# Layer 3's attention in a four-layer kernel: keys before queries, transposes spread between the scores, values two heads behind

## The chip, the cores and the metric

The kernel runs on one NeuronCore of one Trainium2 chip. A NeuronCore has five engines that work side by side and wait for each other by semaphores: TensorE (PE) multiplies matrices and transposes, VectorE (DVE) and ScalarE (ACT) work element by element, GpSimd (POOL) takes odd jobs, and SyncE (SP) issues transfers. PE's products go to PSUM, a small memory of its own, from which DVE and ACT read them. Each engine has a queue of its own, with its instructions in the order in which they were built.

The metric is device time in microseconds (us) for one execution of the whole program. A profiled execution gives the records from which the profile and the trace are made.

## The reference

The reference is four transformer-like layers over 4 sequences of 512 tokens with 256 channels, all in 32-bit floating point. Each layer normalizes its input and adds an attention-like part and a feed-forward part to it. Layer 0 has a state-space mixer and a gated feed-forward, layer 1 a latent attention and a product-key lookup with a gated feed-forward, layer 2 a cheap head-mixing attention and eight small experts, and layer 3 the two parts that this document is about:

```
q = einsum('bpd,hde->bphe', x, W_Q) + b_Q       # 16 heads of 128
k = einsum('bpd,hde->bphe', x, W_K) + b_K
v = einsum('bpd,hde->bphe', x, W_V) + b_V
scores = where(causal, einsum('bqhe,bkhe->bhqk', q, k) / sqrt(128), -1e5)
attn = softmax(scores, axis=-1)
z = einsum('bkhe,bhqk->bqhe', v, attn)
out = einsum('bqhe,hed->bqd', z, W_O) + b_O
```

and a feed-forward of eight experts with 512 hidden units each, in which a router's softmax chooses, per token, the experts whose probabilities add up to 0.9. Here x is the normalized input of the layer.

## The kernel before, in words

The program is written in a tile language: the text allocates named tiles from pools and issues operations to engines, and a scheduler derives the semaphores, may move independent instructions of an engine against each other a little, and gives out the buffers. A pool tag with `bufs=2` has two buffers; a third tile of that tag has to wait until the first has been read for the last time. The PSUM banks are shared by three tags: "mm" with four buffers, "tr" (transposes) with two and "acc" (sums of products) with two.

What is computed concurrently is laid out by `weave`. Every stage is a Python generator that issues some instructions and then yields a number, its estimate of their cost. `weave` always continues the stream that has got the least far in its own total. In `layer3` the attention starts at 0 of its total of 765, and the experts (`top_p_experts`) start at 0.95: so the attention runs nearly alone, its last heads are woven with the experts' routers and first products, and the experts then run alone to the end.

`full_attention` (line numbers are those of the profile) goes through four groups `g` of four heads, and in each through the four sequences `b`. For one `g` and `b`:

- V for four heads is projected in four token tiles (L133, 128x512 each) and copied to SBUF by ACT (L1045).
- For each head, `project_heads` projects the queries and then the keys, each with two products of 512 columns (L125). DVE adds the bias to the queries and scales them (L1002), ACT adds the bias to the keys (L1005).
- `probabilities` is called for four blocks of 128 query tokens. Block i needs the first i+1 blocks of keys, so the score product (L577, in `exp_scores`) is 128, 256, 384 or 512 columns wide. DVE masks and takes each row's minimum in one pass (L580; the queries carry a negative scale, so the minimum is the maximum), ACT takes the exponential and its sum (L584), DVE takes the reciprocal of the sum (L1011) and scales the block (L1012). The tiles are called `pr0` to `pr3`.
- `values` belongs to the head before (the closure `behind`): its probabilities are transposed block by block on PE (L1023: 1, 2, 3 and 4 transposes of 128x128 into one "tr" buffer each), DVE copies each group to the tile PT (L1024), and four products of PT with V (L1027) add up z in an "acc" buffer, which ACT copies to `zT` with a bias (L1031).
- After the fourth head's values, `heads_out` multiplies `zT` by the output weights `wo` in four token tiles of four products each (L593), and DVE adds each to `x` (L142).

In a 32-bit product PE's records come in pairs, with a weight load (PEld) each; a transpose is one record. In the order in which the program before was built, PE does per head: the queries, the first of the keys' two products, the products with V of `values` (for the head two back by now), the second product of the keys, five of the ten transposes of the head before, the four scores, and the other five transposes; the scheduler has moved the pieces of `values` across the projections and the scores.

Of the kernel before, what the change touches and what calls it, by code (L numbers as in the profile page):

```python
# [14 lines left out]
P = 128  # L15
NB, SEQ, DM = 4, 512, 256
NT = NB * SEQ
NTILE = NT // P
TPB = SEQ // P
# [55 lines left out]
def v3(ap, b):  # L75
    return ap.rearrange("p (a b) -> p a b", b=b)
# [45 lines left out]
def project(c, out, w, cols, tokens):  # L122

    for d in range(2):
        c.nc.tensor.matmul(  # L125
            out, lhsT=w[:, d, cols], rhs=c.xnT[:, d, tokens], start=(d == 0), stop=(d == 1)
        )


def project_tokens(c, out, w, cols, tokens):  # L130

    for d in range(2):
        c.nc.tensor.matmul(  # L133
            out, lhsT=c.xnT[:, d, tokens], rhs=w[:, d, cols], start=(d == 0), stop=(d == 1)
        )


def add_scaled(c, t, part, w=None):

    x = c.x[:, t, :]  # L140
    if w is None:
        c.nc.vector.tensor_add(x, part, x)  # L142
    else:
        c.nc.vector.scalar_tensor_tensor(x, part, w, x, ALU.mult, ALU.add)  # L144
# [417 lines left out]
def late_mask(c, pool):  # L562

    late = c.tile(pool, [P, SEQ], "late")
    c.nc.vector.memset(late[:, : SEQ - P], 0.0)
    c.nc.vector.tensor_scalar_mul(late[:, SEQ - P :], c.neg, -1.0)
    return late


def exp_scores(c, pool, late, q, k, i, total, **kw):  # L570

    nc = c.nc
    n = (i + 1) * P
    sc = c.ps()[:, :n]
    nc.tensor.matmul(sc, lhsT=q[:, i * P : n], rhs=k[:, :n], start=True, stop=True)  # L577
    pr = c.tile(pool, [P, n], f"pr{i}", **kw)
    nm = c.tile(pool, [P, 1], "nm", bufs=4)
    nc.vector.tensor_tensor_reduce(  # L580
        out=pr, in0=sc, in1=late[:, SEQ - n :], scale=1.0, scalar=-NEG,
        op0=ALU.add, op1=ALU.min, accum_out=nm,
    )
    nc.scalar.activation(pr, pr, AF.Exp, bias=nm, scale=-1.0, accum_out=total)  # L584
    return pr


def heads_out(c, zT, wo, b):

    for t in range(TPB):  # L590
        po = c.ps("acc")[:, :DM]
        for h in range(4):
            c.nc.tensor.matmul(  # L593
                po, lhsT=zT[:, h, t * P : (t + 1) * P], rhs=wo[:, h, :],
                start=(h == 0), stop=(h == 3),
            )
        add_scaled(c, b * TPB + t, po)
# [5 lines left out]
def latent_pieces(c, a, keep, prep, open_pool):  # L603
# [147 lines left out]
    def turned(s, j):  # L751

        pt = c.ps("tr")
        n = SEQ - j * P
        for i in range(j, TPB):
            nc.tensor.transpose(  # L756
                pt[:, (i - j) * P : (i - j + 1) * P], prs[s][i][:, j * P : (j + 1) * P], c.ident
            )
        copy = nc.scalar.copy if j % 2 else nc.vector.tensor_copy
        return lambda: copy(PTs[s][:, START[j] : START[j] + n], pt[:, :n])  # L760
# [6 lines left out]
    for s in range(65):  # L767
        if s < 64:
            prs[s] = []
        for i in range(TPB):  # L770
            if s < 64:
                probabilities(s, i)
            if s > 0:
                if i == 0:
                    PTs[s - 1] = c.tile(pool, [P, 1280], "PT")
                ready, copy = copy, turned(s - 1, i)
# [200 lines left out]
def full_attention(c, a):  # L977

    nc, tc = c.nc, c.tc
    scale = 128.0 ** -0.5
    with ExitStack() as stack:
        keep, pool = (
            stack.enter_context(tc.tile_pool(name=name, bufs=bufs, side="right"))
            for name, bufs in (("f_keep", 1), ("f_h", 2))
        )
        bias = c.tile(keep, [P, 48 + DM], "bias")
        nc.sync.dma_start(bias, a["f_small"])
        late = late_mask(c, keep)  # L990
        for t in range(NTILE):
            nc.gpsimd.tensor_add(c.x[:, t, :], c.x[:, t, :], bias[:, 48:])

        def project_heads(w3, hh, b):

            wq, wk = w3[:2]
            tokens = slice(b * SEQ, (b + 1) * SEQ)
            cols = slice(hh % 4 * P, (hh % 4 + 1) * P)
            pq, pk = c.ps(), c.ps()
            project(c, pq, wq, cols, tokens)  # L1000
            q = c.tile(pool, [P, SEQ], "q")
            nc.vector.tensor_scalar(q, pq, bias[:, hh : hh + 1], -scale, ALU.add, ALU.mult)  # L1002
            project(c, pk, wk, cols, tokens)
            k = c.tile(pool, [P, SEQ], "k")
            nc.scalar.activation(k, pk, AF.Identity, bias=bias[:, 16 + hh : 17 + hh])  # L1005
            return q, k

        def probabilities(q, k, i):
            rinv = c.tile(pool, [P, 1], "rinv", bufs=4)
            pr = exp_scores(c, pool, late, q, k, i, rinv)  # L1010
            nc.vector.reciprocal(rinv, rinv)  # L1011
            nc.vector.tensor_scalar_mul(pr, pr, rinv)  # L1012
            return pr

        def values(prs, V, h, zT, hh):

            PT = c.tile(pool, [P, TPB, SEQ], "PT")
            for i, pr in enumerate(prs):
                n = (i + 1) * P
                pt = c.ps("tr")  # L1020
                for j in range(i + 1):
                    cols = slice(j * P, (j + 1) * P)
                    nc.tensor.transpose(pt[:, cols], pr[:, cols], c.ident)  # L1023
                nc.vector.tensor_copy(PT[:, : i + 1, i * P : n], v3(pt[:, :n], P))  # L1024
            z = c.ps("acc")
            for j in range(TPB):
                nc.tensor.matmul(  # L1027
                    z[:, j * P :], lhsT=V[:, j, h, :], rhs=PT[:, j, j * P :],
                    start=(j == 0), stop=(j == TPB - 1),
                )  # L1030
            nc.scalar.activation(zT[:, h, :], z, AF.Identity, bias=bias[:, 32 + hh : 33 + hh])  # L1031

        behind = None
        for g in range(4):
            w = c.unit(a["f_units"][g])
            w3 = [v3(w[:, i * 1024 : (i + 1) * 1024], 512) for i in range(3)]
            wo = c.tile(pool, [P, 4, DM], "wo")
            nc.sync.dma_start(wo, v3(a["f_out"][g], DM))
            for b in range(NB):
                V = c.tile(pool, [P, TPB, 4, P], "V")  # L1040
                for t in range(TPB):
                    tt = b * TPB + t
                    pv = c.ps()
                    project_tokens(c, pv, w3[2], slice(0, 512), slice(tt * P, (tt + 1) * P))
                    nc.scalar.copy(V[:, t, :, :], v3(pv, P))  # L1045
                    yield 1.7
                zT = c.tile(pool, [P, 4, SEQ], "zT")
                for h in range(4):
                    hh = 4 * g + h
                    q, k = project_heads(w3, hh, b)  # L1050
                    yield 3.4
                    prs = [probabilities(q, k, i) for i in range(TPB)]
                    yield 2.1
                    if behind:
                        yield behind()

                    def behind(prs=prs, V=V, h=h, zT=zT, hh=hh, wo=wo, b=b, g=g):
                        values(prs, V, h, zT, hh)
                        if h < 3:
                            return 3.2  # L1060
                        heads_out(c, zT, wo, b)
                        if g == 3:
                            c.part_done(b)
                        return 10.0
        behind()

# [147 lines left out]
def layer3(c, a):  # L1216
    weave(c, (full_attention(c, a), 765.0, 0.0), (top_p_experts(c, a), 765.0, 0.95))
# [200 lines left out]
```

## Time and profile before

| what | value |
|---|---|
| time, median of 3 runs (lowest, highest) | 3323.99 us (3313.49, 3325.25) |
| profiled execution: its own time | 3325.63 us |
| profiled execution: its span in the trace | 3323.9 us |
| PE, busy in the span | 3209.1 us (97%), 12524 records |
| DVE, busy in the span | 1894.4 us (57%) |
| ACT, busy in the span | 1255.3 us (38%) |
| layer 3's attention, first to last score (L577) in the trace | 1835.8 to 2676.2 us |
| mean granted TensorE clock | 0.99 |

The span is the time from the first to the last instruction of the profiled execution. A line of the profile's groups names the source line, the engine, the operation, the tiles written and read, the shapes and the number of records. In a timeline each line gives the start, the duration and the records merged into it, and in brackets how long the engine had been idle before and what released it. A table of windows gives the busy time of each engine in each stretch, then the granted clock of TensorE (1.00 is full speed), the share of the DMA engines and GB/s. Matmuls are pipelined, so that a record's end lies over the start of the next one, and the ends are modelled.

### The profile page before, as it was taken

The page shows a single profiled execution, that of the slowest core. Times are in us where ns is not written, and L with a number is a line of the kernel's source. Part 1 is how long each engine was busy: PE and PEld are TensorE (multiplying, and loading weights), DVE is VectorE, ACT ScalarE, POOL GpSimd, SP SyncE. Part 2 cuts the span into 40 slices and gives each one's busy share as a digit, 9 for nine tenths or more (in the row PEclk, how much of TensorE's full clock was granted, in tenths as well). Part 3 has the DMA queues.
Part 4 walks back from the last instruction along what each step waited for, and adds up shares of the span by engine and source line. Part 5 has one row for each costly group of instructions (what it writes and reads, how often), then busy time and mean ns, then how long its engine had stood idle before and what let it go on. Part 6 is the DMA issues. An engine that isn't in the chain of part 4 may idle for free.

```text
span 3323.9 us, 35406 instructions
## 1 busy us (share of the span) xinstructions
PE 3209.1 (97%) x12524; PEld 1921.4 (58%) x12524; DVE 1894.4 (57%) x4720; ACT 1255.3 (38%) x2870; POOL 579.8 (17%) x445
## 2 busy tenths in 40 slices
PE   8999999998899999999999999999999999999999
PEld 4556555655555555455655555556556665555555
DVE  4777778877788678656655545455455532222222
ACT  4444454443565645568322333333333311111111
POOL 0465556655212133100000000000000000000000
PEclk9999999998999999999999999999999999999999
DMA  3233323323213254301001000000000000000000
GB/s 124 77 105 96 125 85 105 102 96 115 59 43 98 50 146 127 90 14 42 15 1 53 5 1 26 0 20 7 0 20 1 1 19 19 20 21 20 17 0 26
DMA packets 75650, 165.14 MB, mean 50 GB/s; under 512 B 12368, under 2 KB 46288, under 8 KB 70608
## 3 DMA queue, kind: packets, MB, share of 16 engines
q1 hardware_dynamic: 64368, 127.20, 11.9%
q0 software_dynamic: 10240, 33.56, 4.1%
q8 instruction: 98, 1.61, 0.2%
q10 hardware_dynamic: 864, 2.12, 0.2%
q14 instruction: 80, 0.66, 0.1%
HBM read 149.08 MB, written 4.85 MB: 46 GB/s over the span
## 4 chain that ended last, share of the span: by engine, by line
PE 72%; DVE 12%; DMA 6%; issue 4%; POOL 4%; ACT 2%; SPq 0%; DVEq 0%; another core or an unknown queue 0%; POOLq 0%; ACTq 0%
PE mm L125 30%; PE acc L194 10%; PE mm L577 7%; PE mm L133 4%; PE acc L1027 4%; PE acc L593 3%; DMA G<-own 3%; DVE cy L259 2%; PE tr L1023 2%; DVE G L400 2%; DMA e<-in_p_experts,ids 2%; PE tr L756 1%; PE acc L813 1%; PE tr L486 1%; PE acc L800 1%
## 5 line engine op out<-in xcount | busy, mean ns | idle before, releaser
L125 PE MATMUL mm<-xnT,wu 128*128 128x512 f32 x2384 | 1083.4, 597 | 9.2 <-DVE cy L259 4.7
L125 PEld LDWEIGHTS mm<-xnT,wu 128*128 128x128 f32 x2384 | 444.8, 191 | 462.9 <-issue 426.4
L584 ACT ACTIVATE pr<-pr,nm 128x128 f32<-128x128 f32 (+3 forms) x512 | 286.6, 560 | 257.9 <-DVE nm L580 234.0
L186 ACT ACTIVATE sg<-mm 128x512 f32<-128x512 f32 x200 | 119.0, 595 | 697.7 <-PE mm L125 697.5
L187 DVE TENSOR_TENSOR hT<-sg,mm 128x512 f32<-128x512 f32 x200 | 136.9, 684 | 424.3 <-PE mm L125 415.3
L194 PE MATMUL acc<-wu,hT 128*128 128x256 f32 x1600 | 374.1, 382 | 0.0
L194 PEld LDWEIGHTS acc<-wu,hT 128*128 128x128 f32 x1600 | 300.7, 191 | 89.4 <-issue 34.8
L580 DVE CUSTOM_DVE_ANT_0 pr<-mm,late 128x128 f32<-128x128 f32 (+3 forms) x512 | 245.5, 486 | 70.4 <-PE mm L577 55.3
L125 PE MATMUL mm<-xnT,w_in 128*128 128x512 f32 x512 | 231.5, 596 | 6.6 <-DVE cy L259 5.1
L144 DVE SCALAR_TENSOR_TENSOR x<-acc,cw,x 128x256 f32<-128x256 f32 x256 | 123.3, 483 | 182.0 <-PE acc L194 177.1
L917 POOL DMA_INDIRECT e<-in_p_experts,ids x128 | 129.8, 1014 | 359.4 <-DVE x L144 315.1
L400 DVE TENSOR_TENSOR_SCAN G<-G,eye 128x1024 f32<-128x1024 f32 x64 | 155.6, 2431 | 56.4 <-DMA G<-own 56.3
L577 PE MATMUL mm<-kf,qf 128*128 128x128 f32 (+3 forms) x512 | 177.7, 448 | 7.8 <-DVE qf L735 4.4
L1024 DVE COPY PT<-tr 128x128 f32<-128x128 f32 (+3 forms) x256 | 118.7, 481 | 107.1 <-PE tr L1023 107.0
L426 POOL TENSOR_TENSOR G<-G,CB 128x1024 f32<-128x1024 f32 x64 | 151.1, 2361 | 142.2 <-ACT CB L352 81.3
L259 DVE SCALAR_TENSOR_TENSOR cy<-mm,ws,cy 128x509 f32<-128x509 f32 (+2 forms) x216 | 158.4, 741 | 28.9 <-ACT cy L255 25.6
L125 PEld LDWEIGHTS mm<-xnT,w_in 128*128 128x128 f32 x512 | 96.6, 191 | 111.0 <-issue 96.9
L412 ACT ACTIVATE xD<-xc,ws 128x128 f32<-128x128 f32 x256 | 84.3, 391 | 197.7 <-POOL y L449 191.7
L142 DVE TENSOR_TENSOR x<-acc,x 128x256 f32<-128x256 f32 x176 | 73.9, 421 | 148.1 <-PE acc L593 121.1
L577 PE MATMUL mm<-k,q 128*128 128x128 f32 (+3 forms) x512 | 154.9, 446 | 0.8 <-ACT k L1005 0.8
L1027 PE MATMUL acc<-PT,V 128*128 128x512 f32 (+3 forms) x512 | 148.8, 434 | 0.0
L1027 PEld LDWEIGHTS acc<-PT,V 128*128 128x128 f32 x512 | 97.4, 190 | 82.6 <-issue 32.7
(247 smaller groups left out, 4601.3 us busy)
## 6 DMA issues: line engine op xcount, KB each, us to landing
G<-own SPq DMA_DIRECT2D x64, 512.0 KB
w_in<-in_m_units SPq DMA_DIRECT2D x16, 1024.0 KB
eb<-since SPq DMA_DIRECT2D x96, 128.0 KB
wu<-in_o_units SPq DMA_DIRECT2D x8, 1536.0 KB
wo<-in_m_units SPq DMA_DIRECT2D x16, 512.0 KB
psw<-pes SPq DMA_DIRECT2D x128, 64.0 KB
wu<-in_g_units SPq DMA_DIRECT2D x4, 1536.0 KB
wu<-in_f_units SPq DMA_DIRECT2D x4, 1536.0 KB
```

The lines of the kernel that those rows point to most:

```text
L125: c.nc.tensor.matmul(out, lhsT=w[:, d, cols], rhs=c.xnT[:, d, tokens], start=(d == 0), stop=(d == 1))
L133: c.nc.tensor.matmul(out, lhsT=c.xnT[:, d, tokens], rhs=w[:, d, cols], start=(d == 0), stop=(d == 1))
L187: nc.vector.tensor_mul(h, sg, pu)
L194: nc.tensor.matmul(po, lhsT=hT[k][:, t * P : (t + 1) * P], rhs=wd[:, k, :], start=(i == 0), stop=(i == per - 1),)
L259: nc.vector.scalar_tensor_tensor(y[:, j:], src[:, : SEQ - j], conv[:, k, 3 - j : 4 - j], y[:, j:], ALU.mult, ALU.add,)
L400: nc.vector.tensor_tensor_scan(flat, flat, eye.rearrange("p h t -> p (h t)"), 0.0, ALU.mult, ALU.add)
L426: nc.gpsimd.tensor_mul(G, G, seqs[b][2][:, t, :][:, None, :].to_broadcast([P, HG, P]))
L577: nc.tensor.matmul(sc, lhsT=q[:, i * P : n], rhs=k[:, :n], start=True, stop=True)
L580: nc.vector.tensor_tensor_reduce(out=pr, in0=sc, in1=late[:, SEQ - n :], scale=1.0, scalar=-NEG, op0=ALU.add, op1=ALU.min, accum_out=nm,)
L584: nc.scalar.activation(pr, pr, AF.Exp, bias=nm, scale=-1.0, accum_out=total)
L917: nc.gpsimd.indirect_dma_start(out=e, out_offset=None, in_=a["p_experts"], in_offset=bass.IndirectOffsetOnAxis(ap=ids[:, t, k : k + 1], ax ...
L1027: nc.tensor.matmul(z[:, j * P :], lhsT=V[:, j, h, :], rhs=PT[:, j, j * P :], start=(j == 0), stop=(j == TPB - 1),)
```

## The change

`project_heads` is split into `keys` and `queries`, which are called in this order. `values` is split too: `turned` transposes one block of one head and has DVE copy it to PT, and what stays in `values` is the four products with V, ACT's copy to `zT` and, after the fourth head, `heads_out`.

Each head's round then runs so: the keys; the queries; the transposes of the last (512 wide) block of the head before; the products with V of the head two back; and then the four blocks' scores, with the transposes of blocks 2, 1 and 0 of the head before after the first, second and third score. The four blocks are no longer issued as one piece: after each the generator yields 0.7, where it yielded 2.1 after all four. The sum of the yields of four heads, with their V and `heads_out`, is 48.4 as before. After the last head what is left of the last two heads is done at the end.

```diff
@@ -991,19 +991,20 @@
         for t in range(NTILE):
             nc.gpsimd.tensor_add(c.x[:, t, :], c.x[:, t, :], bias[:, 48:])
 
-        def project_heads(w3, hh, b):
-
-            wq, wk = w3[:2]
-            tokens = slice(b * SEQ, (b + 1) * SEQ)
-            cols = slice(hh % 4 * P, (hh % 4 + 1) * P)
-            pq, pk = c.ps(), c.ps()
-            project(c, pq, wq, cols, tokens)
+        def queries(w3, hh, b):
+
+            pq = c.ps()
+            project(c, pq, w3[0], slice(hh % 4 * P, (hh % 4 + 1) * P), slice(b * SEQ, (b + 1) * SEQ))
             q = c.tile(pool, [P, SEQ], "q")
             nc.vector.tensor_scalar(q, pq, bias[:, hh : hh + 1], -scale, ALU.add, ALU.mult)
-            project(c, pk, wk, cols, tokens)
+            return q
+
+        def keys(w3, hh, b):
+            pk = c.ps()
+            project(c, pk, w3[1], slice(hh % 4 * P, (hh % 4 + 1) * P), slice(b * SEQ, (b + 1) * SEQ))
             k = c.tile(pool, [P, SEQ], "k")
             nc.scalar.activation(k, pk, AF.Identity, bias=bias[:, 16 + hh : 17 + hh])
-            return q, k
+            return k
 
         def probabilities(q, k, i):
             rinv = c.tile(pool, [P, 1], "rinv", bufs=4)
@@ -1012,25 +1013,38 @@
             nc.vector.tensor_scalar_mul(pr, pr, rinv)
             return pr
 
-        def values(prs, V, h, zT, hh):
-
-            PT = c.tile(pool, [P, TPB, SEQ], "PT")
-            for i, pr in enumerate(prs):
-                n = (i + 1) * P
-                pt = c.ps("tr")
-                for j in range(i + 1):
-                    cols = slice(j * P, (j + 1) * P)
-                    nc.tensor.transpose(pt[:, cols], pr[:, cols], c.ident)
-                nc.vector.tensor_copy(PT[:, : i + 1, i * P : n], v3(pt[:, :n], P))
+        def turned(head, i):
+
+            if head is None:
+                return
+            if i == TPB - 1:
+                head["PT"] = c.tile(pool, [P, TPB, SEQ], "PT")
+            PT, pr, n = head["PT"], head["prs"][i], (i + 1) * P
+            pt = c.ps("tr")
+            for j in range(i + 1):
+                cols = slice(j * P, (j + 1) * P)
+                nc.tensor.transpose(pt[:, cols], pr[:, cols], c.ident)
+            nc.vector.tensor_copy(PT[:, : i + 1, i * P : n], v3(pt[:, :n], P))
+
+        def values(head):
+
+            h, zT = head["h"], head["zT"]
             z = c.ps("acc")
             for j in range(TPB):
                 nc.tensor.matmul(
-                    z[:, j * P :], lhsT=V[:, j, h, :], rhs=PT[:, j, j * P :],
+                    z[:, j * P :], lhsT=head["V"][:, j, h, :], rhs=head["PT"][:, j, j * P :],
                     start=(j == 0), stop=(j == TPB - 1),
                 )
+            hh = head["hh"]
             nc.scalar.activation(zT[:, h, :], z, AF.Identity, bias=bias[:, 32 + hh : 33 + hh])
-
-        behind = None
+            yield 2.1
+            if h == 3:
+                heads_out(c, zT, head["wo"], head["b"])
+                if hh == 15:
+                    c.part_done(head["b"])
+                yield 6.8
+
+        second = last = None
         for g in range(4):
             w = c.unit(a["f_units"][g])
             w3 = [v3(w[:, i * 1024 : (i + 1) * 1024], 512) for i in range(3)]
@@ -1047,22 +1061,25 @@
                 zT = c.tile(pool, [P, 4, SEQ], "zT")
                 for h in range(4):
                     hh = 4 * g + h
-                    q, k = project_heads(w3, hh, b)
-                    yield 3.4
-                    prs = [probabilities(q, k, i) for i in range(TPB)]
+                    head = dict(h=h, hh=hh, b=b, V=V, zT=zT, wo=wo, prs=[])
+                    k = keys(w3, hh, b)
+                    yield 1.7
+                    q = queries(w3, hh, b)
+                    turned(last, 3)
                     yield 2.1
-                    if behind:
-                        yield behind()
-
-                    def behind(prs=prs, V=V, h=h, zT=zT, hh=hh, wo=wo, b=b, g=g):
-                        values(prs, V, h, zT, hh)
-                        if h < 3:
-                            return 3.2
-                        heads_out(c, zT, wo, b)
-                        if g == 3:
-                            c.part_done(b)
-                        return 10.0
-        behind()
+                    if second:
+                        yield from values(second)
+                    for i in range(TPB):
+                        head["prs"].append(probabilities(q, k, i))
+                        if i < 3:
+                            turned(last, 2 - i)
+                        yield 0.7
+                    second, last = last, head
+        turned(last, 3)
+        yield from values(second)
+        for i in range(3):
+            turned(last, i)
+        yield from values(last)
 
 
 
```

## The prediction

> **What bounds the kernel now.** I began with the page's span and busy shares, then cut the span into stretches, then read TensorE's own timeline for one head of the attention, and last the tile PT for who waits on it.
>
> ```profile
> span 3323.9 us, 35406 instructions
> ...
> PE 3209.1 (97%) x12524; PEld 1921.4 (58%) x12524; DVE 1894.4 (57%) x4720; ACT 1255.3 (38%) x2870; POOL 579.8 (17%) x445
> ```
>
> TensorE has the end. The windows show where layer 3's attention lies (us of the stretch, then busy time by engine, then the granted clock):
>
> ```profile
> 1835.00:2600.00 765.00, 754.28 (x2732) 446.57 (x2731) 385.87 (x1325) 277.52 (x667) 0.00 (x0) 1.00 0.02 8
> 2600.00:2620.00 20.00, 20.00 (x88) 16.69 (x88) 7.16 (x26) 5.17 (x9) 0.00 (x0) 0.66 0.00 1
> ```
>
> For 765 us DVE is half idle and PE records 10.7 us of idleness. The change seems to have only that to win. The timeline of one head (start, duration, records) says otherwise:
>
> ```profile
> 2149.80 0.49 PE L1023 MATMUL tr<-con,pr 128*128 128x128 f32 x3
> 2150.45 0.44 PE L1023 MATMUL tr<-con,pr 128*128 128x128 f32 x2 [0.17 <-DVE PT L1024]
> 2150.80 2.43 PE L577 MATMUL mm<-k,q 128*128 128x128 f32 x8
> 2153.06 0.71 PE L1023 MATMUL tr<-con,pr 128*128 128x128 f32 x5
> 2153.60 2.74 PE L125 MATMUL mm<-xnT,wu 128*128 128x512 f32 x6
> 2156.18 2.32 PE L1027 MATMUL acc<-PT,V 128*128 128x512 f32 x8
> 2158.34 1.02 PE L125 MATMUL mm<-xnT,wu 128*128 128x512 f32 x2
> 2159.20 0.49 PE L1023 MATMUL tr<-con,pr 128*128 128x128 f32 x3
> ```
>
> A head takes 2159.20 - 2149.80 = 9.40 us. Read starts against starts. Five transposes on an open road take 2153.60 - 2153.06 = 0.54, 0.109 each. Eight values records take 2158.34 - 2156.18 = 2.16, and the eight score records have the same widths. Against that:
> - three transposes hold the road 0.65 instead of 0.33: 0.32 lost;
> - the next two hold it 0.35 instead of 0.22: 0.13 lost;
> - the scores hold it 2153.06 - 2150.80 = 2.26 instead of 2.16: 0.10 lost.
>
> So 0.55 us of each head is lost, of which the profile records 0.17. PE stands before the fourth transpose because it writes the third block of probabilities into the first one's PSUM buffer (tag "tr" has two) and DVE has not copied that yet; and it stands before the scores because ACT writes k only just before: PE computes k last, and the scores come five transposes later. Who waits on PT (us in total, times):
>
> ```profile
>   PEld tr L1023: 33.8, 95
> ...
>   PE tr L1023: 9.9, 60
> ```
>
> Matmuls of the transposes waited 60 times, their weight loads 95 times. The stall comes in 60 heads of 64: 60 x 0.55 = 33 us, or 1.0% of the span. The rest of a head, 8.85 us, is streaming that the change keeps.
>
> **What the Trainium skill says.** "Perfetto Trace Analysis", section "Tensor Engine Instruction (MATMUL, LD_WEIGHTS)": the end of a matmul record is an estimate. This trace agrees: 0.17 recorded of 0.55 lost. The same page, "Identifying the Most-Contended Engine": a gap that repeats on the saturated engine can mean too few SBUF or PSUM buffers. Here it is the two "tr" buffers, 60 times. "TensorE: Matmul & The Clock Gate", "What's actually happening": the array's clock falls to half after a low-activity window of about 3.4 us and returns after a busy one. The 0.66 above agrees: the routers' 8-column products, 64 in a row but for five transposes, cost (1 - 0.66) x 20 = 6.8 us.
>
> **The change part by part.** The built order of the changed kernel has the same counts of matmuls, DVE and ACT instructions, and SP and POOL issue the same DMAs in the same sequence. So nothing is removed but waits. Only ACT gets more: 76 table loads instead of 70. In the built order PE's head is: first score, three transposes of the head before, second score, two, third score, one, fourth score, keys, queries, four transposes, values of two heads back.
>
> *Keys first, then queries.* Keys end before queries (1.72), four transposes (0.44) and values (2.16) run; ACT's copy of k takes 0.69 and DVE's of q 0.74. Queries end 2.60 before the first score. The wait for k and the late weight load behind it go: 0.13 + 0.10.
>
> *Transposes between scores.* Here I walk DVE's queue, which keeps its order, with zero at the first score's start. Streaming ends on PE: first score 0.22, three transposes 0.55, second 0.98, two 1.20, third 1.84, one 1.95, fourth 2.81, keys 4.53, queries 6.25, four transposes 6.69, values 8.85. In the trace a reader starts 0.20 to 0.26 after PE's end (values end at 2106.95, ACT's zT starts at 2107.15). The durations of the last block, from the DVE and ACT timelines of a head before:
>
> ```profile
> 2111.54 0.68 DVE L580 CUSTOM_DVE_ANT_0 pr<-mm,late 128x512 f32<-128x512 f32 x1
> ...
> 2113.11 0.16 DVE L1011 RECIPROCAL rinv<-rinv 128x1 f32<-128x1 f32 x1
> ...
> 2113.78 0.48 DVE L1012 TENSOR_SCALAR pr<-pr,rinv 128x512 f32<-128x512 f32 x1
> ```
>
> ```profile
> 2112.26 0.72 ACT L584 ACTIVATE pr<-pr,nm 128x512 f32<-128x512 f32 x1 [0.36 <-DVE nm L580]
> 2112.89 0.19 ACT L584 ACTIVATION_READ_ACCUMULATOR pr<-pr,nm 128x1 f32 x1
> ```
>
> DVE's order in the built kernel, with start-to-start spacings of that timeline: minimum of score 1 at 0.42; copy of three transposes 0.85; reciprocal 1.31 (its exponential ends at 1.25); minimum 2 at 1.39; scale 1 at 1.82; copy of two 2.02; minimum 3 at 2.31; reciprocal 2.79; copy of one 2.87; scale 2 at 3.09; minimum 4 at 3.36; reciprocal 3.97; scale 3 at 4.17. The last exponential starts 0.72 after its minimum (2112.26 - 2111.54), at 4.08; its reciprocal follows 0.85 later at 4.93, the scale at 5.13, done at 5.61. The "tr" buffers: the single transpose (1.84) needs the copy of three, done at 1.39; the four (6.25) need the copy of two, done by 2.4. Both are free. The 0.32 goes.
>
> *The wait this adds.* The four transposes need the last scaled block: ready at 5.61, their weight load comes 0.4 before 6.25, so 0.2 to 0.6 is left; I take 0.4. Queued behind them on PE are the values of two heads back and then all of the next scores, so any lateness is paid in full. Before, this block was transposed only after the next head's scores, so the tightness is new.
>
> *Values two heads behind.* Their PT was copied a whole round earlier, so they don't wait. Two PT buffers, two of each pr, V and zT are enough: each is read before the second next is written. Under heads_out the fourth product of a token needs zT: ACT has it 0.2 + 0.69 = 0.9 after values, PE reaches it after six records of 0.216 = 1.3. Nothing.
>
> *The last stretch*, where the experts are woven in. The finer pieces change the mix. (a) The routers come in four groups of 16 records (16 x 0.111 = 1.8 us) with a score and a few transposes between. The trace of before shows no such mix. Bounds: the clock doesn't fall, 6.8 won; or it falls for five windows instead of four, 1.7 lost, and router results that hold PSUM until DVE comes to them stop PE by another 1 to 2. I take the same four windows: nothing. (b) Six more table loads of 1.28 us on ACT, 7.7 in all, put an exponential late by about one load in three heads. Hidden wholly where PE has an expert's two products (3.4 us) in between; exposed wholly 7.7. I take 2.
>
> Sum: 3323.9 - 33.3 + 2 = 3292.6 for the profiled execution. That execution itself took 3325.6 against a median of 3324.0, so the same 31 us from the median gives 3293.
>
> **The rivals.**
> *The last block's wait takes part of the place.* If DVE or ACT is 0.65 us later than in the walk, the slack of 0.4 is gone and 0.25 a head stays: 60 x 0.25 = 15, so 3308. For it: minimum 4 starts at 3.36 though its score allows 3.01, so DVE is already the later one. Against it: DVE is busy half of the stretch (385.87 of 765).
> *The last stretch eats a fourth.* All table loads exposed (+5.7 over mine), one window more at half clock (1.7) and PSUM held (2): 3302. For it: in the built order ACT goes exp, silu, exp within one head's scores. Against: only four heads.
> *Slower.* The place is DVE's queue: each of the four reciprocals waits for ACT with copies and minimums behind it. If these waits bite in turn, the chain from score to scaled block grows. At 0.4 + 0.55, say 1.0 us a head, all is given back; at 1.5 it costs 60 x 0.55 = 33 beyond: 3357. For it: strict order, and the interleaved copies stand before the last minimum. Against: in the walk three of the four reciprocals find their exponential finished.
> *It doesn't do what it says*: a scheduler stands between text and engines and could have undone it: 3324. The built order shows it carried out, so this is small.
>
> **How the numbers follow.** Stalls gone 0.65, at 3293 (own range 3283 to 3299: clock kept, or loads exposed); last stretch dear 0.15, 3302; part of the wait stays 0.13, around 3308; slower 0.05, about 3357; no effect 0.02. A measurement here can tell about 0.5% (16.6 us; the three runs span 3313 to 3325), so faster means below 3307: 0.65 + 0.15 + 0.08 = 0.88; within 0.02 + 0.05 = 0.07; slower 0.05. Range 3280 to 3308: the low end is the kept clock (3286) with the spread of the runs, the high end the second rival.
>
> **What will show it.** In the changed profile a head should take 8.85 us start to start (the 13.8 us for V, 16 records of 0.43, and heads_out, 32 of 0.216, in every fourth stay); PE's waits for PT before transposes (60 times) should be gone, and the scores take 2.16 when the transposes between are counted out. A PE gap before the four transposes, released by the scale line (pr), says the second rival. A clock of 1.00 around the routers says 3286. I am wrong if PE shows a new repeated gap between scores.

## The result and the profile after

| what | before | after |
|---|---|---|
| time, median (lowest, highest) | 3320.49 us of 4 runs (3313.49, 3325.25) | 3288.74 us of 4 runs (3287.72, 3290.41) |
| profiled execution: its own time, its span | 3325.63, 3323.9 us | 3290.41, 3288.6 us |
| first score (L577) of layer 3 to the last PE record | 1484.3 us | 1452.8 us |

The ratio is 0.9902, with a 95% interval of 0.9885 to 0.9919: 31.8 us less between the medians. The forecast was 3293 us, inside 3280 to 3308. The two profiled executions lie 35.3 us apart in their spans. From the first score on it is 31.5; the other 3.7 are from the layers ahead, whose code is the same and whose length varies from run to run (in the runs of this study layer 3's first score comes between 1823 and 1836 us). The experiments below are therefore compared by the time from the first score to the last PE record where a few us matter.

The page of the changed kernel, its span and its busy times:

```profile
span 3288.6 us, 35510 instructions
...
PE 3185.0 (97%) x12524; PEld 1918.6 (58%) x12524; DVE 1886.5 (57%) x4720; ACT 1258.2 (38%) x2876; POOL 573.6 (17%) x445
```

The same records on PE, six more instructions on ACT (the table loads). The busy share stays at 97%: as before, it tells nothing. The windows of the changed kernel (busy time and records by engine, then the granted clock):

```profile
1835.00:2560.00 725.00, 724.83 (x2703) 438.62 (x2702) 375.39 (x1307) 265.78 (x653) 0.00 (x0) 1.00 0.03 9
2560.00:2600.00 40.00, 40.00 (x154) 28.76 (x153) 22.22 (x79) 11.92 (x21) 0.00 (x0) 0.79 0.00 1
```

The recorded idleness has gone from 10.7 us in 765 to 0.2 in 725. Around the routers the clock is lower: (1 - 0.79) x 40 = 8.4 us, where before it was 6.8. PE's timeline of one head after:

```profile
2164.48 0.60 PE L1026 MATMUL tr<-con,pr 128*128 128x128 f32 x4
2164.91 2.32 PE L1034 MATMUL acc<-PT,V 128*128 128x512 f32 x8
2167.07 0.39 PE L577 MATMUL mm<-k,q 128*128 128x128 f32 x2
2167.30 0.49 PE L1026 MATMUL tr<-con,pr 128*128 128x128 f32 x3
2167.62 0.60 PE L577 MATMUL mm<-k,q 128*128 128x256 f32 x2
2168.06 0.38 PE L1026 MATMUL tr<-con,pr 128*128 128x128 f32 x2
2168.28 0.81 PE L577 MATMUL mm<-k,q 128*128 128x384 f32 x2
2168.92 0.27 PE L1026 MATMUL tr<-con,pr 128*128 128x128 f32 x1
2169.03 1.02 PE L577 MATMUL mm<-k,q 128*128 128x512 f32 x2
2169.89 3.60 PE L125 MATMUL mm<-xnT,wu 128*128 128x512 f32 x8
2173.32 0.60 PE L1026 MATMUL tr<-con,pr 128*128 128x128 f32 x4
```

From one group of four transposes to the next it is 2173.32 - 2164.48 = 8.84 us, where it was 9.40. Every step has its open-road length: four transposes 0.43, eight values records 2.16, scores 0.23, 0.44, 0.64 and 0.86, the three groups of transposes between them 0.32, 0.22 and 0.11. Summed over 1835 to 2530 us PE loses 0.2 us against such spacings (0.110 us for a record of 128 columns, 0.216 for 256, 0.323 for 384 and 0.4295 for 512), where before it lost 30.9 in 1835 to 2560. Who waited for the tile PT after, between 1835 and 2700 us (us in total, times):

```profile
  ACT zT L1039: 225.4, 64
  PEld tr L1026: 0.9, 2
  PEld acc L1034: 0.2, 1
```

The matmuls of the transposes, which waited 60 times, are no longer in the list.

### The profile page after: what moved, and what is told of

It reads as the page before. It is cut to its first block, busy times and chain, and to the rows that moved or that the text cites. A ratio compares the mean times of both kernels' runs of the same rounds, so it can differ in the third digit from the quotient of the medians.

```text
span 3288.6 us, 35510 instructions
## 1 busy us (share of the span) xinstructions
PE 3185.0 (97%) x12524; PEld 1918.6 (58%) x12524; DVE 1886.5 (57%) x4720; ACT 1258.2 (38%) x2876; POOL 573.6 (17%) x445
## 4 chain that ended last, share of the span: by engine, by line
PE 73%; DVE 11%; DMA 6%; issue 4%; POOL 3%; ACT 2%; SPq 0%; DVEq 0%; ACTq 0%; POOLq 0%
PE mm L125 31%; PE acc L194 10%; PE mm L577 7%; PE mm L133 5%; PE acc L1034 4%; PE acc L593 3%; DMA G<-own 2%; DMA e<-in_p_experts,ids 2%; PE tr L1026 2%; DVE cy L259 2%; DVE G L400 2%; PE tr L486 2%; PE tr L756 1%; PE acc L813 1%; PE acc L800 1%
## 5 line engine op out<-in xcount | busy, mean ns | idle before, releaser
L577 PE MATMUL mm<-kf,qf 128*128 128x128 f32 (+3 forms) x512 | 175.7, 444 | 5.9 <-DVE qf L735 2.2
L577 PE MATMUL mm<-k,q 128*128 128x128 f32 (+3 forms) x512 | 179.1, 439 | 1.1 <-issue 0.9
L999 DVE TENSOR_SCALAR q<-mm,bias 128x512 f32<-128x512 f32 x64 | 48.0, 751 | 170.1 <-PE mm L125 170.1
L486 PE MATMUL tr<-wo,y 128*128 128x256 f32 x512 | 131.5, 402 | 8.4 <-DVE xdt L408 2.9
```

The source lines that it names most:

```text
L486: nc.tensor.matmul(po, lhsT=y[:, k, :], rhs=groups[i][1][:, k, :], start=(k == 0), stop=(k == 3))
```

## The experiments

The first question was which part of the change earns the 31 us: the prediction gave 0.32 us a head to the buffer (the transposes between the scores), 0.13 + 0.10 to the order of keys and queries, and nothing to the values. In the expectations, A is the theory held at the time and B its rival; every text says what each is. The experiments ran on three chips, on which the kernel before takes 3323.37, 3316.31 and 3313.45 us; so ratios and traces are compared, and not times in us across chips.

**Keys first alone.** The kernel before, with the three lines for k ahead of those for q:

```diff
-            pq, pk = c.ps(), c.ps()
-            project(c, pq, wq, cols, tokens)
-            q = c.tile(pool, [P, SEQ], "q")
-            nc.vector.tensor_scalar(q, pq, bias[:, hh : hh + 1], -scale, ALU.add, ALU.mult)
+            pk, pq = c.ps(), c.ps()
             project(c, pk, wk, cols, tokens)
             k = c.tile(pool, [P, SEQ], "k")
             nc.scalar.activation(k, pk, AF.Identity, bias=bias[:, 16 + hh : 17 + hh])
+            project(c, pq, wq, cols, tokens)
+            q = c.tile(pool, [P, SEQ], "q")
+            nc.vector.tensor_scalar(q, pq, bias[:, hh : hh + 1], -scale, ALU.add, ALU.mult)
```

> The kernel before with one edit: the keys are projected before the queries. Theory A (the loss of 0.55 us a head is two overlapping waits, for a transpose buffer and for the last projection's copy, and only work between that projection and the scores can hide the second): the late operand is now q, which DVE writes 0.2 + 0.75 + 0.05 = 1.0 us after its last product, with only three transposes (0.33 us) in between, so 0.67 + 0.10 us a head are lost instead of 0.55 and the time rises by 60 x 0.22 = 13 us, to some 3334 from 3321. Theory B (the split by parts in the prediction, keys first alone wins 0.23 us a head): 14 us less, some 3307.

Measured: 3339.44 us beside 3323.37 for the kernel before, ratio 1.0052 (1.0036 to 1.0069); first score to end 1499.0 us, 14.7 more than before, or 16.4 if it is counted that the clock around the routers stood at a half for 10.24 us instead of 13.65. This part alone makes the kernel slower. PE's timeline in it:

```profile
2153.55 1.02 PE L125 MATMUL mm<-xnT,wu 128*128 128x512 f32 x2
2154.41 0.49 PE L1023 MATMUL tr<-con,pr 128*128 128x128 f32 x3
2155.41 2.42 PE L577 MATMUL mm<-k,q 128*128 128x128 f32 x8 [0.52 <-DVE q L1005]
```

and who waited for the tile q in it, between 1835 and 2600 us:

```profile
  PE mm L577: 34.6, 59
```

Only three transposes (0.33 us) now stand between the projections and the scores, and the scores' matmuls waited for q 59 times. Here they start 1.00 us after the projections ended (1.10 in three heads of four), 0.67 of it empty. The wait for k has only changed its name.

**A buffer of its own for the third block alone.** The kernel before, with the transposes of block 2 going to an "acc" buffer, so that none of the four groups waits for the first one's copy:

```diff
-                pt = c.ps("tr")
+                pt = c.ps("acc" if i == 2 else "tr")
```

> The kernel before with one edit: the three transposes of the third block go to a buffer of the tag acc instead of tr, so that they needn't wait for the first block's copy. Theory A (two overlapping waits): the buffer wait goes, but then PE reaches the scores after seven transposes (0.76 us) and k is there only 1.0 us after its last product: 0.24 + 0.10 us a head stay, 0.21 are won, 60 x 0.21 = 13 us less, some 3308. Theory B (the split by parts: the buffer alone is 0.32 us a head): 19 us less, some 3302.

Measured: 3305.98 us, ratio 0.9948 (0.9931 to 0.9964); 1467.7 us from the first score, 16.6 less. Of these 3.4 come from the routers (the clock stood at a half for 6.83 us instead of 13.65), so the edit itself is worth 13. PE's timeline in it:

```profile
2152.64 0.49 PE L1023 MATMUL tr<-con,pr 128*128 128x128 f32 x3
2152.97 0.49 PE L1023 MATMUL acc<-con,pr 128*128 128x128 f32 x3
2153.30 0.33 PE L1023 MATMUL tr<-con,pr 128*128 128x128 f32 x1
2153.64 2.43 PE L577 MATMUL mm<-k,q 128*128 128x128 f32 x8
```

Seven transposes now run without a stop (0.66 for the first six), and yet the scores start 1.00 us after the projections, as they did before with five transposes and a stop among them. The buffer's stall lay inside a wait for k that was there anyway. ACT's timeline of the kernel before, at the head that the prediction shows, has that wait too:

```profile
2150.05 0.69 ACT L1005 ACTIVATE k<-mm,bias 128x512 f32<-128x512 f32 x1 [7.14 <-PE mm L125]
```

The keys' products end at 2149.80, where the transposes start, ACT's copy of k ends at 2150.74, and the scores start at 2150.80. What the edit gains is that the scheduler now puts two more transposes into that wait: 2 x 0.109 = 0.22 a head, 60 x 0.22 = 13.

**Both together, in the old order.** The two edits above in one kernel.

> The kernel before with both edits of the two runs above. Theory A: q is the late operand, 1.0 us after its last product, with six transposes (0.65 us) in between: 0.35 + 0.10 us a head stay, 0.10 are won, 6 us less, some 3315. Theory B (the parts add up): all 0.55 us a head are won, 33 us less, some 3288, as the changed kernel.

Measured: 3316.11 us, ratio 0.9981 (0.9973 to 0.9990); 1480.8 us from the first score, 3.5 less than before. If the prediction's parts had been separate causes this would have brought all 33 us. PE's timeline in it:

```profile
2161.14 0.49 PE L1023 MATMUL tr<-con,pr 128*128 128x128 f32 x3
2161.47 0.49 PE L1023 MATMUL acc<-con,pr 128*128 128x128 f32 x3
2162.24 2.40 PE L577 MATMUL mm<-k,q 128*128 128x128 f32 x8 [0.28 <-DVE q L1005]
```

**Queries first in the changed kernel.** Everything else as changed:

```diff
-                    k = keys(w3, hh, b)
-                    yield 1.7
                     q = queries(w3, hh, b)
+                    yield 1.7
+                    k = keys(w3, hh, b)
```

> The changed kernel with one edit undone: queries first, then keys. Theory A: the keys' copy on ACT now has the four transposes and the values (2.6 us) to hide in, as the queries' had, so nothing changes: 3289 within 2. Theory B (keys first is a working part of the change, 0.23 us a head): 14 us more, 3303.

Measured: 3291.77 us, ratio 0.9911 (0.9895 to 0.9928); 1449.5 us from the first score, 3.3 less than the changed kernel, of which the routers explain 3.4 (10.24 us at half clock instead of 17.07). In the new order it makes no difference which of the two comes first.

**Values one head behind.** The changed kernel, with the values of the last head after the fourth score, instead of those of the second last ahead of the scores:

```diff
...
-                    if second:
-                        yield from values(second)
                     for i in range(TPB):
                         head["prs"].append(probabilities(q, k, i))
                         if i < 3:
                             turned(last, 2 - i)
                         yield 0.7
-                    second, last = last, head
+                    if last:
+                        yield from values(last)
+                    last = head
...
```

> The changed kernel with the values one head behind instead of two: they are issued after the fourth score of the next head, and no longer stand between the projections and the scores. In the built order PE goes from the queries straight to seven transposes (0.76 us) and then to the first score. Theory A (what hides q's copy is the values between projection and scores): q is there 1.0 us after its last product, so 0.24 + 0.10 us a head are lost, 20 us more than the changed kernel, some 3309. Theory B (the lag of two only lets PT be copied in time, and one behind is enough): 3289 within 3.

Measured: 3305.06 us beside 3316.31 for the kernel before, ratio 0.9970 (0.9959 to 0.9980); 1475.3 us from the first score, 24.2 more than another run of the changed kernel with the same 13.65 us at half clock (1451.1). Most of the gain is gone. PE's timeline in it:

```profile
2150.01 2.74 PE L125 MATMUL mm<-xnT,wu 128*128 128x512 f32 x6
2152.59 0.93 PE L1026 MATMUL tr<-con,pr 128*128 128x128 f32 x7
2153.69 0.89 PE L577 MATMUL mm<-k,q 128*128 128x128 f32 x4 [0.17 <-DVE q L999]
```

The transposes are free of stops and three of the ten still stand between scores, and the scores wait all the same: 2153.69 - 2152.59 = 1.10 us after the projections.

**One rule for the five.** Over all heads of 1840 to 2500 us whose projections end directly ahead of such a group, the time from the end of the projections to the first score has these medians; the lost time is the difference, and 0.07 to 0.10 more follow, in all but the changed kernel, behind a weight load that comes late:

| kernel | projected last, copied by | end of projections to first score, us | PE's work in between, us | lost, us |
|---|---|---|---|---|
| before | keys, ACT | 1.00 (52 heads) | 5 transposes, 0.55 | 0.45 |
| keys first alone | queries, DVE | 1.10 (51 heads) | 3 transposes, 0.33 | 0.77 |
| other buffer alone | keys, ACT | 1.00 (53 heads) | 7 transposes, 0.76 | 0.24 |
| both | queries, DVE | 1.10 (51 heads) | 6 transposes, 0.65 | 0.45 |
| values one behind | queries, DVE | 1.10 (51 heads) | 7 transposes, 0.76 | 0.34 |
| changed | queries, DVE | 2.60 (41 heads) | 4 transposes and the values, 2.60 | 0 |

So in the first five one wait sets the time, and not three: the operand that is projected last needs 1.00 or 1.10 us until the scores can read it, and what counts is how much other work PE has in that time. Keys last is even 0.10 better than queries last. The values, 2.16 us that wait for nothing, are longer than that by themselves. It is their place that counts and not their lag: in the built order of the kernel before they belonged to the head two back as well, but stood ahead of the keys' second product, and so covered the queries' copy and not the keys'. What no run tests is the values in their new place with the transposes still in one piece; whether the full "tr" buffer would then show a stall of its own stays open.

The second question was the wait that the change adds. By the prediction the four transposes' block is ready about 0.4 us early, and any lateness beyond that is paid in full. **The last block scaled again,** by 1.0 (more work on DVE, the same values), once in the first kernel and three times, with `range(3)`, in the second:

```diff
             nc.vector.tensor_scalar_mul(pr, pr, rinv)
+            if i == TPB - 1:
+                for _ in range(1):
+                    nc.vector.tensor_scalar_mul(pr, pr, 1.0)
```

> The changed kernel with the last block scaled once more, by 1.0, on DVE: it lengthens the chain from the fourth score to its transposes by some 0.45 us. In the trace of the changed kernel that block is ready 0.34 us before its first weight load and 0.76 us before its first transpose. Theory A (the slack is that of the transpose, 0.7): nothing, 3289 within 3. Theory B (it is that of the weight load, 0.34): 0.1 to 0.2 us a head, 6 to 12 us more.

> The changed kernel with the last block scaled three times more, by 1.0: the chain grows by some 1.35 us. Theory A (slack 0.7): 0.65 to 0.8 us a head are lost, 60 x 0.7 = 42 us more, some 3331, slower than the kernel before, which is the rival of the prediction that ends on the slower side. Theory B (PE has other work to put in between, or the slack is far larger than read): 3289 within 5.

Measured: 3283.21 us, ratio 0.9900 (0.9884 to 0.9917), and 1451.1 us from the first score with one more scaling; 3286.31 us, 0.9909 (0.9883 to 0.9935), and 1452.2 us with three. No loss in either: A held for the first and fell for the second, where it expected 42 us. PE's timeline with three more scalings:

```profile
2181.79 1.67 PE L1037 MATMUL acc<-PT,V 128*128 128x512 f32 x4
2183.29 0.60 PE L1029 MATMUL tr<-con,pr 128*128 128x128 f32 x4
2183.73 0.82 PE L1037 MATMUL acc<-PT,V 128*128 128x256 f32 x4
```

Here the scheduler has put the first half of the values ahead of the four transposes. The values need nothing of the block that these wait for, so they can stand on either side, and the block has 1.5 us more. Of every four heads this is so in one; in two the first quarter of the values (0.86 us) stands ahead; and in the fourth the products of V stand ahead of the projections anyway. To see the price without that, **the same with the order held**: the transposes and the products of the values are marked so that PE keeps them, among themselves, in the order of the text. The scores stay free.

```diff
-                nc.tensor.transpose(pt[:, cols], pr[:, cols], c.ident)
+                tc.keep_in_program_order(nc.tensor.transpose(pt[:, cols], pr[:, cols], c.ident))
...
-                nc.tensor.matmul(
+                tc.keep_in_program_order(nc.tensor.matmul(
                     z[:, j * P :], lhsT=head["V"][:, j, h, :], rhs=head["PT"][:, j, j * P :],
                     start=(j == 0), stop=(j == TPB - 1),
-                )
+                ))
```

> As the run with the last block scaled three times more, but the transposes and the values are held in the order in which the text issues them, which that run had not kept: there the scheduler had put two or more of the values products before the four transposes, and nothing was lost. In the built order 45 heads now have the four transposes directly after the projections, as the changed kernel has; in 15 two scores stand before them. Theory A (in a fixed order the slack is 0.76 us and lateness beyond it is paid in full): the block is ready 1.35 us later, or 2.1 where DVE takes q's copy in between, so 0.6 to 1.3 us are lost in each of some 45 heads, 27 to 58 us more than the changed kernel: 3316 to 3347. Theory B (the slack itself is far larger than read from the trace): 3289 within 5.

Measured: 3320.96 us beside 3313.45, ratio 1.0024 (1.0016 to 1.0033): slower than before. From the first score 1490.5 us, 39.4 more than the changed kernel run beside it (1451.1). PE's timeline in it:

```profile
2180.95 3.60 PE L125 MATMUL mm<-xnT,wu 128*128 128x512 f32 x8
2185.15 0.63 PE L1029 MATMUL tr<-con,pr 128*128 128x128 f32 x4 [0.61 <-DVE pr L1016]
...
2197.50 3.60 PE L125 MATMUL mm<-xnT,wu 128*128 128x512 f32 x8
2202.03 0.89 PE L577 MATMUL mm<-k,q 128*128 128x128 f32 x4 [0.94 <-DVE q L999]
...
2207.52 3.60 PE L125 MATMUL mm<-xnT,wu 128*128 128x512 f32 x8
2211.52 0.63 PE L1029 MATMUL tr<-con,pr 128*128 128x128 f32 x4 [0.40 <-DVE pr L1016]
```

In the first of these heads the transposes come 4.20 us after the projections began instead of 3.43: 0.77 lost. Three scalings take 1.35, so 1.35 - 0.77 = 0.58 us were free. But the 39 us are of two kinds. The trace repeats with every four heads: in one, behind V's products, nothing is lost; in one the block is late by 0.77, in one by 0.57; and in one, the second that is shown, the scores of two blocks now stand directly behind the projections, and the scores wait for q's copy with nothing in between, 1.10 and 0.07 behind it. That is 15 x (0.77 + 0.57) = 20 us for the late block and 15 x 1.17 = 18 for q. The total lies inside A's range, but A had put nothing down for the 15 heads with the scores ahead, and a third of its 45 heads, those behind V, lost nothing. So lateness of the block does have a price, which the order that the scheduler chose in the run before kept away; and the operand's copy, left without cover, costs as much here as the lateness itself.

The third question was the clock around the routers. **Routers apart:** the experts' stream starts earlier and yields 12.0 instead of 1.0 after each router, so that more than a head's work lies between two of them:

```diff
-            yield 1.0
+            yield 12.0
...
-    weave(c, (full_attention(c, a), 765.0, 0.0), (top_p_experts(c, a), 765.0, 0.95))
+    weave(c, (full_attention(c, a), 765.0, 0.0), (top_p_experts(c, a), 765.0, 0.89))
```

> The changed kernel with the four routers set about a head apart (their generator yields 12.0 instead of 1.0, and its stream starts at 0.89 instead of 0.95). The same work. Theory A (the clock falls to half because four routers in a row leave windows of 3.4 us with little array work; in the changed kernel for 17 us, which costs 8.5): with one router of 1.8 us at a time the clock stays at full speed, and 7 to 9 us are won, some 3281. Theory B (a single router is enough to drop the clock): each costs its own half-clock window of 3.4 us or more, nothing won or some us lost, 3287 to 3296.

> The changed kernel with the four routers a head apart, again, beside the changed kernel itself. Theory A (the half clock around the routers is what this wins): 6 to 9 us less than the changed kernel on the same chip, and a clock of 1.00 throughout the attention. Theory B (the first measurement lay on the lucky side of the runs' spread): within 3 us of the changed kernel.

> The changed kernel once more, beside the next run on the same chip: 0.990 of the kernel before, and TensorE at half clock for 10 to 17 us around the four routers.

Measured: 3274.94 us beside 3316.31 for the kernel before, ratio 0.9879 (0.9862 to 0.9895), and again 3277.66 beside 3313.45, 0.9889 (0.9871 to 0.9907). The changed kernel on the same chip as the second had 3282.82, 0.9904 (0.9889 to 0.9920). From the first score it is 1444.4 us in both runs against 1451.1: 6.7 less, and the half clock of 13.65 us, which costs half of that, 6.8, is gone. The medians lie 5.2 apart, and the intervals of the ratios overlap, so the traces carry this and not the times. By the spacings given above, PE loses 39.8 us from the first score on in the kernel before, 6.6 in the changed kernel of that run, and none here: what is left of layer 3 is TensorE's own work. The windows that hold the four routers (they start at 2503.8, 2519.4, 2531.3 and 2547.0):

```profile
2500.00:2520.00 20.00, 20.00 (x96) 14.81 (x95) 11.67 (x40) 4.69 (x12) 0.00 (x0) 1.00 0.00 1
2520.00:2540.00 20.00, 20.00 (x92) 12.77 (x92) 16.19 (x67) 7.70 (x21) 0.00 (x0) 1.00 0.00 0
2540.00:2560.00 20.00, 20.00 (x82) 12.07 (x81) 11.90 (x44) 7.48 (x18) 0.00 (x0) 1.00 0.00 1
```

The clock is 1.00 in all of them. This is the fastest kernel of the study.

## Why the prediction was right, and where it was not

**What bounds it, and how much is lost.** Right. Reading starts against starts gave 0.55 us a head in 60 heads and 8.85 us for what remains; the changed kernel shows 8.84, and the sum from the first score is -31.5 where the steps gave -33.3 + 2 = -31.3.

**"The wait for k and the late weight load behind it go: 0.13 + 0.10" and, under the transposes, "The 0.32 goes".** They went, but the split is the step that failed. The three pieces were read as three stalls, one for each edit to remove. The runs show one wait of 1.00 us behind the keys; in the kernel before, the full "tr" buffer only decided at which place in it PE stood. So keys first alone costs 15 to 16 us where the split gives it 14 of gain, the buffer alone brings 13 where the split gives 19, and both together bring 3.5 and not 33. The forecast came out all the same because the change makes all the edits at once, so that the split does not enter the sum. The prediction had taken from the Trainium skill ("Perfetto Trace Analysis", where the sentence stands in the section "Optimization Strategy" and not in the one that it names) that a gap that repeats can mean too few buffers. Here there was a full buffer, 60 times, but the measurement decides: with a buffer more (the other buffer alone) the scores still came 1.00 us after the keys.

**"Values two heads behind": "Nothing".** No cost, as argued; but without this part most of the gain is gone, because it puts 2.16 us between the last projection and the first score. With the values one head behind 0.34 + 0.07 us a head came back, 24.2 us in all. That it would earn the gain without the spread transposes is not shown. The number was in the prediction's own working ("Queries end 2.60 before the first score"), booked to the order of keys and queries, which is worth nothing in the new order.

**"The transposes between scores" by the walk along DVE.** Right. The last block was to be ready 5.61 us after the first score. In DVE's timeline of the changed kernel:

```profile
2171.88 0.16 DVE L1012 RECIPROCAL rinv<-rinv 128x1 f32<-128x1 f32 x1 [0.35 <-ACT pr L584]
2172.08 0.48 DVE L1013 TENSOR_SCALAR pr<-pr,rinv 128x512 f32<-128x512 f32 x1
```

it is ready at 2172.56, 5.49 after 2167.07, and in that of the weight loads

```profile
2172.90 0.14 PEld L1026 LDWEIGHTS tr<-con,pr 128*128 128x128 f32 x1 [0.24 <-issue]
```

its load comes 0.34 later. The slack was taken as 0.4 out of 0.2 to 0.6; the kernel with the order held shows that 0.58 could be used, or 1.35 - 0.57 = 0.78 in the heads that follow the odd order.

**"Any lateness is paid in full."** It holds where the order is held: 0.77 of 1.35 paid, which is all beyond the 0.58. Where the scheduler was free, it answered the same lateness with another order, and nothing was paid. But it orders the program when it is built, and could do so because the extra scalings stand in the text. Lateness that only the chip brings, as the rival meant it (DVE or ACT slower than in the walk), would have met the order as built, with the four transposes first; no run tests that, and the trace shows the block 0.34 us early instead.

**The last stretch: two terms mis-sized, with opposite signs.** The table loads were taken as 2 us exposed. In the changed kernel they lie at 2583 to 2653 us, and from 2581 to 2670 us PE lost 0.1 us in all. The clock was taken as unchanged. It was the bound named beside it, "five windows instead of four, 1.7 lost". PE's timeline of the changed kernel there:

```profile
2560.43 1.85 PE L133 MATMUL mm<-wr,xnT 128*128 128x8 f32 x16
...
2562.77 2.57 PE L133 MATMUL mm<-wr,xnT 128*128 128x8 f32 x16
...
2566.61 3.42 PE L133 MATMUL mm<-wr,xnT 128*128 128x8 f32 x16
...
2571.52 3.42 PE L133 MATMUL mm<-wr,xnT 128*128 128x8 f32 x16
...
2576.64 4.05 PE L1034 MATMUL acc<-PT,V 128*128 128x512 f32 x6
```

Sixteen router records take 1.85 in the first group and 3.42 in the last two, and the values behind them are still slow. By the trace's clock records the clock stood at a half for 17.07 us, five times 3.41, and before for 13.65, four times: (17.07 - 13.65) / 2 = 1.7. So the sum should have been -33.3 + 1.7 + 0 = -31.6. That it also came out at -31.3 is luck of two errors of the same size; and in another run of the changed kernel the clock fell for 13.65 us, so this term is not fixed.

## What to carry to other kernels

Two waits of one engine that lie one behind the other need not add up: before giving each its edit, take the end of the last producer and the start of the first reader, and ask what the next wait would be if this one were gone. An operand's copy through another engine is a latency to be covered, and the work that covers it best is work that waits for nothing, as products a round behind; which operand is made first mattered here only while that cover was too small. Lateness that is written into a program which a scheduler orders is not priced until its built order has been looked at, since filler that may stand on either side moves; and an order that is held to measure one wait can lay another bare.

## What the hardware did that was not expected

The time from the last product of a projection to the first product that reads its copy was nearly constant over some fifty heads: 1.00 us through ACT (whose copy takes 0.69) and 1.10 through DVE (0.75), with three to seven transposes in between or, in 15 heads of the kernel with the order held, with nothing.

Around the 8-column products of the routers the clock fell here only when these came close together. The Trainium skill ("TensorE: Matmul & The Clock Gate", "What's actually happening") gives an idle window of about 3.4 us as what throttles the array. The runs agree with that size: the times at half clock around the routers were 6.83, 10.24, 13.65 and 17.07 us, all multiples of 3.41. They do not show idleness: in the 20 us of before at a clock of 0.66 PE is recorded busy for all 20.00. With four router groups within 15 us the time at half clock was never none, in eleven traces; with one group of 1.85 us in every 12 to 16 us it was none, in two. That the low activity of such narrow products is what the hardware counts is argued from this and not shown by itself. Nor is it settled why the same program had four windows in one run and five in another.
